# Attention: transposes of the negated maxima ahead of the matmuls for the sums of the weights

## The chip, the cores and the metric

The kernel runs on one core of one Trainium2 chip. The metric is the device time of one execution, in microseconds. The kernel before takes 1847.09 us in the median of 3 runs (1846.87 to 1848.96).

## What is computed

Two layers work on 2 x 1024 tokens of width 512, in fp32. Each adds an attention part and a feed-forward part to the normalised input. Only the second layer's attention matters here. It has 16 heads of width 32 and a causal mask:

```python
def _L1_attn_ref(x, W_qkv, b_qkv, W_out, b_out):
    ...
    qkv = x @ W_qkv.T + b_qkv
    q, k, v = jnp.split(qkv, 3, axis=-1)
    ...
    scores = jnp.einsum('bqhe,bkhe->bhqk', q, k) * scale
    causal = jnp.tril(jnp.ones((l, l), dtype=bool))
    scores = jnp.where(causal[None, None], scores, -jnp.inf)
    attn = jax.nn.softmax(scores, axis=-1)
    out = jnp.einsum('bhqk,bkhe->bqhe', attn, v)
    out = out.reshape(b, l, d)
    out = out @ W_out.T + b_out
    return out
```

## The kernel before

The kernel has three stages: the first layer (about 0 to 723 us), the second layer's attention (723 to 1230), and the second layer's feed-forward (to the end).

Attention works in 8 units, one for each batch and each group of four heads. The scores are computed twice. The first pass, `maxima` (L1033), puts queries on partitions: it multiplies q and k in PSUM pair tiles `m` (L1042, four heads, two heads to a pair), adds the mask on the diagonal (L1049) and takes the row maxima on VectorE (L1050). `shift_part` (L1062) negates the maxima on ScalarE and splits them into three bf16 parts, with GpSimd forming what is left. `shift_rows` (L1074) turns the parts around with four bf16 transposes on TensorE into the PSUM tile `px` (L1080), which VectorE copies to SBUF as `neg` (L1084).

The second pass, `weights` (L1086), puts keys on partitions: it multiplies k and q into the pair tiles `s` (L1095), adds the negated maxima with a three-row bf16 matmul of ones (L1101), takes the exponential on ScalarE into `pt` or `acc` (L1112), and sets what lies above the diagonal to zero on GpSimd (L1117). `gather` (L1126) multiplies the values with it into `o` (L1137, one group of 32 array columns per head) and adds `pt` onto `acc` on GpSimd (L1145, on VectorE near the end). `total` (L1152) sums `acc` over the keys with matmuls of ones into the PSUM tile `w` (L1157, again one group of 32 columns per head), and ScalarE copies it to `inv` (L1162). `divide` (L1164) takes reciprocals on VectorE in four quarters (L1167), and GpSimd multiplies the attention output with them (L1169).

`s`, `m`, `w` and `px` all come from `ps_wide`, a rotation of three PSUM tiles of two banks each. A tile's writer waits until the reader of the tile three places earlier in the rotation is done. A step without `w` and `px` takes s, s, m, m; one with both takes s, s, w, px, m, m.

The order of work is written out by hand in one loop (L1300). A unit has 12 steps n: four for the first half of the queries, eight for the second. Each step issues the second pass for its key block, what `put_mid` has noted for it, `gather` for the step before, what `put_after` has noted for it, the first pass for 13 steps ahead (`ahead`), and a part of a projection (`one_part`: two matmuls out of `pq`, `pv` or `po`, L990). `in_program_order` (L48) then holds TensorE, VectorE, ScalarE and GpSimd to the order of that list. `put_after` appends to a list for a step, and the list is worked off in the order in which it was filled:

```python
            for f, *args in after.pop(n, ()):
                f(*args)
```

`shift_rows` is noted at the steps 12u - 5 and 12u + 3, `total` at 12u + 7 and 12u + 15. So they meet in 14 steps: at 12u + 7 `total(u, 0)` with `shift_rows(u + 1, 0)`, and at 12u + 3 `total(u - 1, 1)` with `shift_rows(u, 1)`. In the step 12u + 7 the scores are 512 queries wide; in the step 12u + 3 they are 128 wide, and the `o` of the step before is 256 wide. In all of these steps but the last (in unit 7) a first pass 512 keys wide follows.

Of the kernel before, what the change touches and what calls it, by code (L numbers as in the profile page):

```python
# [35 lines left out]
def two_layers(ctx: ExitStack, tc: tile.TileContext, t: dict, out: bass.AP):  # L36
# [307 lines left out]
    with tc.tile_pool(name="a", bufs=1) as a:  # L344
# [415 lines left out]
        for n in range(NU - 1):  # L760
            u = 2 * n + 2
# [24 lines left out]
        for q, n in enumerate(((0, 2), (0, 4), (1, 2), (1, 4))):  # L786
            put0(*n, fwht_rows, q)
            for m in range(4):
                n, at = (0, (4, 5, 6, 6)[m]) if q == 0 else divmod(4 * q + 3 + m, 7)
# [101 lines left out]
        n, second_half = NU - 1, list(products_of(NU - 1, 1))  # L891
# [14 lines left out]
    with tc.tile_pool(name="b", bufs=1, reuse_waits="tile") as b:  # L906
# [91 lines left out]
        def project(u, m, n):  # L998


            bb, hg = units[u]

            def done(pq):
                if (u, m) not in qk:
                    qk[u, m] = b.tile([P, S], F32, tag=f"qk{m}", name=f"qk{m}_{u}", bufs=3)
                nc.scalar.activation(  # L1006
                    qk[u, m][:, n * TT : (n + 1) * TT], pq, AF.Identity,
                    bias=bqk[:, m * HG + hg : m * HG + hg + 1],
                )

            return piece(
                f"pq_{u}_{m}_{n}", lambda k: wqk[hg][:, k, m, :],
                lambda k: xt1[2 * bb + n][:, k, :], done,
            )

        def values(bb, n, j):


            def done(pv):
                if (bb, n, j) not in vals:  # L1020
                    vals[bb, n, j] = b.tile(
                        [P, D], F32, tag="v", name=f"v_{bb}_{n}_{j}", bufs=12
                    )
                nc.vector.tensor_add(vals[bb, n, j], pv, bv)

            return piece(
                f"pv_{bb}_{n}_{j}", lambda k: xt1[2 * bb + n][:, k, j * P : (j + 1) * P],
                lambda k: wv[:, k, :], done,
            )
# [170 lines left out]
        def put(n, *what):  # L1200
            fixed.setdefault(n, []).append(what)

        def put_mid(n, *what):

            middle.setdefault(n, []).append(what)

        def put_after(n, *what):

            after.setdefault(n, []).append(what)

        for u in range(len(units)):

            for half in range(2):
                n = per * u - ahead + (3, 11)[half]
                if half:
                    put(n + 1, larger, u)
                for m in range(3):
                    put_mid(n + 2 + m, shift_part, u, half, m)
                put_after(n + 5, shift_rows, u, half)
            if u:  # L1220
                lo = per * (u - 2) if u > 1 else -ahead
                for x in range(4):
                    rest.append((lo, per * u - ahead - 1, project(u, x // 2, x % 2)))
            if u > 1:
                put(per * (u - 2) - 1, load_qk, units[u][1])
            for j in range(2):
                n = per * u + 8 * j + 7
                if n < len(second):
                    put_after(n, total, u, j)
                    for q in range(4):  # L1230
                        put(n + q * 2 // 3, divide, u, j, q)
                else:
                    put(len(second) + 2, total, u, j)
        for x in range(4):
            rest.append((-ahead, x, values(0, 0, x)))
            rest.append((-ahead, 7 + x, values(0, 1, x)))
            for j in range(2):
                put(2 * x + j - 12, last_stats, 2 + x // 2, 2 * (x % 2) + j)
                put(2 * x - 9, last_row, 2 + x // 2, 2 * (x % 2) + j)
            put(2 * x - 10, last_norm, 2 + x // 2, x % 2)  # L1240
            rest.append((per, per * 4 + x, values(1, 0, x)))

            rest.append((per * 3 + 5 + x, per * 4 + 2 + x, values(1, 1, x)))
# [77 lines left out]
        n = len(second)  # L1321
# [14 lines left out]
    with tc.tile_pool(name="c", bufs=1, reuse_waits="tile") as c_:  # L1336
# [127 lines left out]
        for n in range(groups - 1):  # L1464

            end = n == groups - 2
            u = 2 * n + 2
# [22 lines left out]
        n = groups - 1  # L1490
# [144 lines left out]
```

## Time and profile before

| | |
|---|---|
| median of 3 runs | 1847.09 us (1846.87 to 1848.96) |
| the profiled execution | 1850.59 us |
| its span, first to last instruction | 1848.78 us |
| mean granted TensorE clock | 0.994 |
| matmuls of `w`, L1157 | 128 of 0.592 us (16 times `total`) |
| transposes into `px`, L1080 | 64 of 0.219 us (16 times `shift_rows`) |
| copy of `w` on ScalarE, L1162 | 16 of 0.585 us |
| copy of `px` on VectorE, L1084 | 16 of 0.424 us |
| exponential of a full pair, L1112 | 1.02 us |
| maxima of a full pair, L1050 | 1.22 us |

How to read the profile: PE is the matmul side of TensorE and PEld its weight loads, DVE is VectorE, ACT ScalarE, POOL GpSimd. A row of the timeline has the start in us from the span's start, the length in us, the engine, the line, the operation with the tile it writes and those it reads, the shape, and the number of instructions merged. A bracket gives the idle time of the engine before it and what ended it. An fp32 matmul is listed as two passes, so four heads give x8. Matmuls overlap: the time that a group holds TensorE is the distance from its start to the start of the next group, which is shorter than the row's length.

### The profile page before, as it was taken

Reading aid. Unit: us, or ns where it says so; the run is one execution under the profiler, and the core shown is the slowest. Engines: PE = TensorE matmul, PEld = TensorE weight load, DVE = VectorE, ACT = ScalarE, POOL = GpSimd, SP = SyncE. Lnnn points to the kernel's source line nnn. Section 1 sums busy time; section 2 is a strip of 40 time slices with the busy share of each in tenths; the row PEclk is TensorE's granted clock in tenths of the full one; section 3 lists DMA queues with packets and bytes.
Section 4 is the critical chain, followed back from the end, with each engine's and each line's share of the span. In section 5 each row is a group of like instructions: output and inputs, shape, how many; then the busy total and the mean of one; then the engine's idle time right before and its main releaser. Section 6 shows DMA issues by size and latency. Waiting matters only on the chain.

```text
span 1848.8 us, 18896 instructions
## 1 busy us (share of the span) xinstructions
PE 1798.2 (97%) x7348; PEld 918.6 (50%) x7348; DVE 1127.4 (61%) x1464; ACT 478.5 (26%) x683; POOL 821.1 (44%) x711
## 2 busy tenths in 40 slices
PE   6999999999999999999999999999999999999999
PEld 4446565655655564333333333333455555555544
DVE  3685444565543438565657656642768678768665
ACT  2322222122221102334333443412211221212120
POOL 4335364246552222467667756732244244343410
PEclk9999999999999999999999999999999999999999
DMA  6121111011101100000001000011101101211101
GB/s 228 35 80 34 35 35 38 31 46 35 35 23 34 35 7 23 1 12 12 13 1 35 12 12 1 24 46 34 35 23 57 57 23 58 91 35 46 46 1 46
DMA packets 29465, 68.12 MB, mean 37 GB/s; under 512 B 3392, under 2 KB 11584, under 8 KB 27840
## 3 DMA queue, kind: packets, MB, share of 16 engines
q1 hardware_dynamic: 28656, 66.61, 10.9%
q8 instruction: 59, 0.97, 0.2%
q10 hardware_dynamic: 720, 0.30, 0.1%
q14 instruction: 30, 0.25, 0.0%
HBM read 62.70 MB, written 4.19 MB: 36 GB/s over the span
## 4 chain that ended last, share of the span: by engine, by line
PE 88%; DVE 5%; POOL 2%; ACT 2%; issue 2%; DMA 1%; ACTq 0%; POOLq 0%; DVEq 0%
PE p_a L179 20%; PE p_c L179 19%; PE d L297 19%; PE pq L990 6%; PE m L1042 4%; PE s L1095 4%; PE o L1137 3%; PE po L990 3%; PE pv L990 3%; PE dr L1454 2%; POOL acc L1145 2%; PE w L1157 1%; DVE tops L1050 1%; PE pp L579 1%; PE s L1101 1%
## 5 line engine op out<-in xcount | busy, mean ns | idle before, releaser
L315 POOL TENSOR_TENSOR x<-x,de 128x512 f32<-128x512 f32 x87 | 125.9, 1462 | 298.4 <-DVE x L310 163.7
L1145 POOL TENSOR_TENSOR acc<-acc,pt 128x1024 f32<-128x1024 f32 (+3 forms) x138 | 233.7, 1719 | 0.0
L1050 DVE TENSOR_REDUCE tops<-m 128x2 f32<-128x1024 f32 (+2 forms) x192 | 180.8, 956 | 49.1 <-PE m L1042 44.7
L310 DVE TENSOR_TENSOR x<-x,d 128x512 f32<-128x512 f32 x145 | 99.3, 685 | 149.8 <-PE d L297 148.6
L1112 ACT ACTIVATE pt<-s 128x1024 f32<-128x1024 f32 (+3 forms) x160 | 115.1, 766 | 180.3 <-PE s L1101 167.1
L297 PE MATMUL d<-td,h 128*128 128x256 f32 x592 | 139.9, 380 | 2.2 <-DVE h L272 2.2
L297 PEld LDWEIGHTS d<-td,h 128*128 128x128 f32 x592 | 112.2, 190 | 46.2 <-issue 29.0
L990 PE MATMUL pq<-xt,wqk 128*128 128x512 f32 x256 | 125.1, 617 | 0.8 <-ACT qk L1006 0.8
L179 PE MATMUL p_a<-t_a,s_a 128*128 128x512 f32 x256 | 119.2, 610 | 2.1 <-DVE t_a L156 2.1
L179 PE MATMUL p_a<-xt,w 128*128 128x512 f32 x256 | 117.7, 603 | 0.7 <-ACT xt L136 0.7
L179 PE MATMUL p_c<-xt,s_c 128*128 128x512 f32 x256 | 115.2, 593 | 2.5 <-DVE e_c L224 1.4
L179 PE MATMUL p_a<-xt,s_a 128*128 128x512 f32 x256 | 116.6, 598 | 0.0
L179 PE MATMUL p_c<-xt,gu 128*128 128x512 f32 x256 | 114.9, 592 | 0.0
L179 PE MATMUL p_c<-t_c,s_c 128*128 128x512 f32 x256 | 114.6, 592 | 0.0
L1049 DVE TENSOR_TENSOR m<-m,mask 128x256 f32<-128x256 f32 x128 | 54.7, 427 | 98.2 <-PE m L1042 93.7
L1042 PE MATMUL m<-qk,qk 32*128 32x512 f32 (+3 forms) x768 | 107.7, 536 | 3.6 <-ACT acc L1112 3.0
L1095 PE MATMUL s<-qk,qk 32*128 32x512 f32 (+3 forms) x768 | 93.8, 532 | 3.7 <-ACT pt L1112 2.3
L172 POOL TENSOR_TENSOR s_c<-gu,s_c 128x512 f32<-128x512 f32 x16 | 20.4, 1275 | 135.9 <-PE p_c L179 135.9
L1117 POOL TENSOR_SCALAR_AFFINE_SELECT pt<-pt 128x256 f32<-128x256 f32 x112 | 48.4, 448 | 71.2 <-ACT pt L1112 70.6
L990 PEld LDWEIGHTS pq<-xt,wqk 128*128 128x128 f32 x256 | 44.5, 191 | 66.5 <-issue 62.1
L179 PEld LDWEIGHTS p_a<-xt,s_a 128*128 128x128 f32 x256 | 47.2, 190 | 57.1 <-issue 56.7
L179 PEld LDWEIGHTS p_c<-xt,s_c 128*128 128x128 f32 x256 | 48.5, 190 | 54.2 <-issue 52.9
(240 smaller groups left out, 3049.2 us busy)
## 6 DMA issues: line engine op xcount, KB each, us to landing
w<-in_W SPq DMA_DIRECT2D x32, 512.0 KB, 3.6
gu<-in_gu SPq DMA_DIRECT2D x32, 512.0 KB, 3.6
wd<-in_down SPq DMA_DIRECT2D x8, 1024.0 KB, 4.8
x<-in_x SPq DMA_DIRECT2D x16, 256.0 KB, 4.2
w2h<-in_W2q SPq DMA_DIRECT2D x4, 1024.0 KB, 11.7
xr<-in_x SPq DMA_DIRECT2D x16, 256.0 KB, 2.7
wqk<-in_WqkvT SPq DMA_DIRECT2D x16, 256.0 KB, 3.2
out_x<-x SPq DMA_DIRECT2D x16, 256.0 KB, 2.0
```

Source lines behind the costliest of these rows:

```text
L179: nc.tensor.matmul(pair[:, m, :], a[:, m, k, :], x[:, k, :], start=start and k == 0, stop=stop and k == 1, skip_group_check=True,)
L297: nc.tensor.matmul(out_[:, j, :], lhs[:, q, j * P : (j + 1) * P], rhs[:, q], start=m in (0, 1, 3, 4) and j == q == 0, stop=j == q == 1, sk ...
L310: nc.vector.tensor_add(r, r, out_)
L315: nc.gpsimd.tensor_add(r, r, u2[half])
L990: nc.tensor.matmul(got[0], lhs(k), rhs(k), start=(k == 0), stop=(k == KC - 1))
L1042: nc.tensor.matmul(pair[h // 2][:, h % 2, :e], q[rows, qt * P : (qt + 1) * P], k[rows, c * 512 : c * 512 + e], start=True, stop=True,)
L1049: nc.vector.tensor_add(d, d, mask.unsqueeze(1).to_broadcast([P, 2, P]))
L1050: nc.vector.tensor_reduce(out=tops[u][:, c, qt, 2 * p : 2 * p + 2], in_=pair[p][:, :, :e], axis=mybir.AxisListType.X, op=ALU.max,)
L1095: nc.tensor.matmul(pair[h // 2][:, h % 2, s:], k[rows, kt * P : (kt + 1) * P], q[rows, cols], start=True, stop=False,)
L1112: nc.scalar.activation(pt[:, :, s:], pair[p][:, :, s:], AF.Exp, scale=1.0 / math.sqrt(HD))
L1137: nc.tensor.matmul(po[rows, s:], v[:, rows], pts[h // 2][:, h % 2, s:], start=(kt == 0), stop=last, tile_position=(0, h * HD),)
L1145: eng.tensor_add(acc[:, :, s:], acc[:, :, s:], pt[:, :, s:])
```

## The change

`total` is no longer noted while the units are walked through. It is collected in a list, and noted for its steps after all `shift_rows` are. In a step that has both, `shift_rows` is now issued first and `total` behind it. Steps that have one of the two stay as they are, and the steps themselves are the same. With the order, the places in the rotation of PSUM tiles change: such a step takes s, s, px, w, m, m.

```diff
+        sums_at = []
         for u in range(len(units)):
 
             for half in range(2):
...
             for j in range(2):
+
                 n = per * u + 8 * j + 7
                 if n < len(second):
-                    put_after(n, total, u, j)
+                    sums_at.append((n, total, u, j))
                     for q in range(4):
                         put(n + q * 2 // 3, divide, u, j, q)
                 else:
                     put(len(second) + 2, total, u, j)
+        for what in sums_at:
+            put_after(*what)
```

## The prediction

> **What bounds the kernel now.** I read the page first, for the busy engine and the chain that ended last.
>
> ```profile
> span 1848.8 us, 18896 instructions
> PE 1798.2 (97%) x7348; PEld 918.6 (50%) x7348; DVE 1127.4 (61%) x1464; ACT 478.5 (26%) x683; POOL 821.1 (44%) x711
> PE 88%; DVE 5%; POOL 2%; ACT 2%; issue 2%; DMA 1%; ACTq 0%; POOLq 0%; DVEq 0%
> ```
>
> TensorE is busy for 97% of the span and carries 88% of the chain. So a microsecond saved in its queue counts, unless another engine is the limit at that place. Then the busy time by stretch, inside attention (723 to 1230 us):
>
> ```profile
> 860.00:920.00 60.00, 59.01 (x400) 21.27 (x397) 37.37 (x53) 22.41 (x36) 40.80 (x43) 1.00 0.03 10
> 920.00:980.00 60.00, 59.01 (x399) 21.25 (x396) 36.08 (x51) 23.92 (x38) 40.79 (x42) 1.00 0.04 10
> ```
>
> The columns after the length are PE, PEld, DVE, ACT and POOL. One unit of four heads lasts about 61 us, PE is busy for 59.0 of 60, and POOL, the next, for 40.8. PE's own short stalls are hidden in that busy time, because matmuls overlap and a pair that waits lies under its neighbour. They have to be read from starts. So I took the timeline at the two kinds of step that hold both w and px. First the wide one (query rows 512 wide), then the narrow one (scores only 128 wide), and then an ordinary step without either.
>
> ```profile
> 783.83 1.06 PE L1137 MATMUL o<-pt,v 128*32 128x512 f32 x8
> 784.71 1.04 PE L1157 MATMUL w<-acc,ones 128*32 128x512 f32 x8
> 785.68 0.40 PE L1080 MATMUL px<-identb,parts 128*128 128x128 bf16 x4
> 785.82 0.59 ACT L1162 COPY inv<-w 128x512 f32<-128x512 f32 x1
> 786.01 1.57 PE L1042 MATMUL m<-qk,qk 32*128 32x512 f32 x8
> 786.12 0.42 DVE L1084 COPY neg<-px 128x512 bf16<-128x512 bf16 x1 [3.33 <-PE px L1080]
> 787.51 1.98 PE L990 MATMUL pq<-xt,wqk 128*128 128x512 f32 x4
> ```
>
> ```profile
> 824.82 1.07 PE L1157 MATMUL w<-acc,ones 128*32 128x512 f32 x8 [0.48 <-DVE tops L1050]
> 825.82 0.40 PE L1080 MATMUL px<-identb,parts 128*128 128x128 bf16 x4
> 825.94 0.58 ACT L1162 COPY inv<-w 128x512 f32<-128x512 f32 x1 [1.50 <-PE w L1157]
> 826.15 1.56 PE L1042 MATMUL m<-qk,qk 32*128 32x512 f32 x8
> 827.64 1.98 PE L990 MATMUL pq<-xt,wqk 128*128 128x512 f32 x4
> ```
>
> ```profile
> 795.75 1.07 PE L1137 MATMUL o<-pt,v 128*32 128x512 f32 x8
> 796.75 1.15 PE L1042 MATMUL m<-qk,qk 32*128 32x512 f32 x8
> 797.83 1.98 PE L990 MATMUL pv<-wv,xt 128*128 128x512 f32 x4
> ```
>
> What to see: m of the same shape (eight passes of 512) holds PE from its start to the next group's start for 797.83 - 796.75 = 1.08 us where nothing is in its way. It takes 787.51 - 786.01 = 1.50 us in the wide step and 827.64 - 826.15 = 1.49 in the narrow one. The cause is the rotation of three PSUM pairs. A step takes s, s, w, px, m, m in that order, so the second m pair gets the buffer of the tile that stands first after s, which is w. It waits for ScalarE's copy of w, which ends at 785.82 + 0.59 = 786.41 (narrow: 826.52), although m could have had it at 786.01. That is 0.42 us (narrow 0.41) of bare wait on the bottleneck engine.
>
> **The change part by part.** The program orders of the two kernels, laid side by side, differ in PE alone: in 14 steps the four transposes of px come ahead of w's matmuls. No instruction is added, and DVE, ACT, POOL and the DMA queue keep theirs in order. Of the 14 steps, 7 are wide (PE's w at 784.71 and then each 62 us), 6 narrow (824.82 and so on), and one is a narrow one in the tail (1190).
>
> 1. The second m pair now takes px's buffer and waits for VectorE's copy of px. In the wide step px starts in w's place after o. Behind o an instruction of another array shape starts 796.75 - 795.75 = 1.00 after o's start, so px starts at 784.83. The copy starts 786.12 - 785.68 = 0.44 later and takes 0.42, so it ends at 785.69. VectorE stood idle for 3.33 us before that copy, so it is free. m needs the buffer only at about 786.16, and the copy is covered by w's matmuls with 0.47 us to spare. The stall of 0.42 goes.
>
> 2. The price is the order o, px, w, m. Here a rule speaks against the change. The row: px starts 785.68 - 784.71 = 0.97 after w in the wide step, and w starts only 784.71 - 783.83 = 0.88 after o, while m behind o takes 1.00. So w right behind o gets in 0.12 early, since both use 32-column groups. The Trainium skill (TensorEngine Tiling (Array Packing), Key Properties) says that changing the tiling mode drains TensorE, changing the tile within one mode doesn't. Before, o and w share a mode and px and m are one change each. After, px stands between o and w, one more drain in each wide step. The rule gives no price; the rows do: 0.12 for w's lost early start, and 0.03 for its first weight load (w holds 1.00 in the narrow step, where it starts on a drained array, against 0.97). So o 1.00, px 0.33 (786.01 - 785.68), w 1.00: m starts at 783.83 + 2.33 = 786.16, 0.15 later than now, and the next group at 787.24 in place of 787.51: -0.27. If the drain were free it would be -0.42. A w group directly behind a bf16 transpose is not in this trace. The nearest row is m behind px, 0.33, and I take it. A gain below nothing is excluded since the number of changes grows; from above, all eight weight loads of w bare, 8 x 0.110 us (the group of w's LDWEIGHTS) = 0.88, is the worst.
>
> 3. In the narrow step px, not w, is what waits for the preceding maxima on VectorE, at the same 824.82. The array is drained there anyway. px 0.33 and w 1.00 put m at 826.15 as today, and 0.41 goes whole.
>
> 4. The wait that takes the removed one's place is on the next step's first score pair: it now gets w's buffer. ScalarE's copy starts 1.11 us after w (785.82 - 784.71), so 785.16 + 1.11 + 0.59 = 786.86. The scores come at 789.43 - 0.27 = 789.16. m (1.08) and pq (1.91) cover it with 2.3 us; without pq there are still 0.4. ScalarE idles 4.49 us ahead of its next exponential, so nothing is queued behind the later copy. The second score pair waits for the first maximum, at most 0.15 later (about 788.55), also in time. The reciprocals come behind both maxima and move with them.
>
> 5. The tail step has no m. There the second score pair is the one that waits for w's copy: s holds 1.70 us against 1.29 elsewhere. The same sum gives -0.28, but the reciprocals, and VectorE's sums behind them, start about 0.4 later, so between -0.28 and +0.2. I take -0.2, nearer the PE rows.
>
> What the saved time runs into: POOL's sums form a closed queue after each wide step, but that queue begins with a mask that waits for an exponential (POOL idle 6.9 us before it at 792), and the exponential waits for scores on PE. It starts earlier by as much as PE. The wait for maxima ahead of the narrow step starts from m on PE as well.
>
> Sum: 7 x 0.27 = 1.9, 6 x 0.41 = 2.5, tail 0.2: 4.6 us. The profiled execution took 1850.59 us (span 1848.78), so it would be 1846.0. It lies 3.5 above the median of the runs, 1847.09; taken from that, 1842.5.
>
> **Rivals.**
> - The saving is absorbed. What speaks for it: PE waits 0.48 us for VectorE's maxima ahead of each narrow step, and POOL's queue reaches up to an o in the first unit. If the wide steps' 1.9 stayed there, only 2.7 are left: 1844.4. Against it: both queues start from PE, as above.
> - Slower, by the drain: if w behind a transpose must load all its weights bare, each of the 14 steps pays 0.88, or 12.3, against 4.6 saved: 1854.8. It decides from 0.33 us per step upward (4.6 / 14). Against it: m behind the same transposes starts in 0.33, with its loads run ahead.
> - The change doesn't do what it says: m's second pair really waits for the exponential of its step. Then the extra drains stay, 7 x 0.15: 1848.1. Against it: in the wide step that exponential ended at 785.86 and in the narrow one at 824.45, long before the pair moved, while the copy's end fits both.
>
> **How the numbers follow.** About 0.2%, 3.7 us, is what a measurement of this kernel can tell from no change. Forecast 0.70, absorbed 0.16, drain 0.09, no effect 0.05. The forecast's own spread is some 1 us. The runs lie 2.1 apart, and a stretch of 3.4 us at a granted clock of 0.51 (809.2 in this trace) costs about 0.7 on the pq it hits (2.57 for 1.91); where it falls may differ. So of 0.70, 0.62 lies under 1843.4; with a little of the absorbed case faster is 0.65, the same 0.25, slower 0.10. The range goes from 1841.0 (drain free, 7 x 0.15 more, and half a microsecond of spread) to 1846.0, which takes in the absorbed case and leaves out the other two.
>
> **What would show it.** In the profile after, px at about 1.00 behind o in the wide steps, w 0.33 behind px, m 1.08 in place of 1.50 in both kinds, the copy of w behind m's start, and the scores without a wait for that copy. It is wrong if w starts later than 0.4 behind px, if m still holds 1.5, or if a new gap of some 0.3 us opens ahead of the scores, of o, or of the next narrow step's px.

## The result

The changed kernel takes 1844.52 us in the median of 14 runs (1841.11 to 1846.34), the kernel before 1847.95 beside it (14 runs, 1846.87 to 1849.49). The ratio is 0.9979, with a 95% interval of 0.9971 to 0.9987: 3.4 us gained. In a second session it took 1843.59 in the median of 10 runs, at a ratio of 0.9974 (0.9965 to 0.9983).

The profiled execution took 1841.11 us with a span of 1839.4, 9.4 less than the one of before. That is more than the runs differ by, and more than the change is worth, so the page's span must not be read as the effect. First the page, then the two kinds of step.

```profile
span 1839.4 us, 18901 instructions
PE 1788.5 (97%) x7348; PEld 911.7 (50%) x7348; DVE 1122.8 (61%) x1464; ACT 478.6 (26%) x683; POOL 820.1 (45%) x711
```

The wide step after, in the timeline:

```profile
782.21 1.07 PE L1137 MATMUL o<-pt,v 128*32 128x512 f32 x8
783.20 0.40 PE L1080 MATMUL px<-identb,parts 128*128 128x128 bf16 x4
783.53 1.06 PE L1157 MATMUL w<-acc,ones 128*32 128x512 f32 x8
783.64 0.42 DVE L1084 COPY neg<-px 128x512 bf16<-128x512 bf16 x1 [2.47 <-PE px L1080]
784.53 1.14 PE L1042 MATMUL m<-qk,qk 32*128 32x512 f32 x8
784.66 0.58 ACT L1162 COPY inv<-w 128x512 f32<-128x512 f32 x1 [0.42 <-PE w L1157]
785.60 1.98 PE L990 MATMUL pq<-xt,wqk 128*128 128x512 f32 x4
```

The copy of px ends at 784.06, before m starts, and the copy of w runs beside m. The row of m has shrunk from 1.57 to 1.14, and m holds PE for 785.60 - 784.53 = 1.07 us where it held 1.50. From the start of o to that of px it takes 0.99 where it took 0.88 from o to w, and w starts 0.33 behind px. From o to pq the step takes 3.39 us, before 787.51 - 783.83 = 3.68: 0.29 less. The narrow step after:

```profile
820.41 0.64 PE L1137 MATMUL o<-pt,v 128*32 128x256 f32 x8
821.53 0.38 PE L1080 MATMUL px<-identb,parts 128*128 128x128 bf16 x4 [0.48 <-DVE tops L1050]
821.84 1.06 PE L1157 MATMUL w<-acc,ones 128*32 128x512 f32 x8
822.84 1.14 PE L1042 MATMUL m<-qk,qk 32*128 32x512 f32 x8
823.91 1.98 PE L990 MATMUL pq<-xt,wqk 128*128 128x512 f32 x4
```

Now px bears the wait of 0.48 for VectorE's maxima that w bore, m again holds 1.07, and from the first of the pair to pq it takes 2.38 in place of 827.64 - 824.82 = 2.82: 0.44 less. In the view of waits of PE over attention, w stood before and px stands after, and no other line has grown:

```profile
PE w L1157 <- DVE tops L1050: 2.9, 6, 0.5
PE px L1080 <- DVE tops L1050: 0.5, 1, 0.5
```

```profile
PE px L1080 <- DVE tops L1050: 3.4, 7, 0.5
PE m L1042 <- ACT acc L1112: 3.0, 8, 0.7
```

All 7 wide and all 6 narrow steps read the same to 0.02 us. From one wide step to the next a unit takes 61.10 us after (841.20 to 902.30, from the scores' start) and 61.83 before (844.93 to 906.76). The 0.73 are the 0.29 and the 0.44 of the two steps, so nothing is taken back in between.

**Where the other 4.6 us of the profile come from.** Both traces contain stretches of 3.4 us, or twice that, at half the granted clock. The stretch table of before and of after, at three such places and at one without (the eighth field is the granted clock):

```profile
809.20:812.65 3.45, 3.45 (x18) 1.70 (x19) 1.23 (x3) 2.18 (x4) 3.45 (x6) 0.51 0.00 0
1215.40:1218.85 3.45, 3.45 (x8) 1.17 (x4) 1.90 (x4) 0.00 (x0) 1.29 (x2) 0.51 1.01 425
```

```profile
806.00:810.00 4.00, 3.76 (x31) 1.54 (x24) 2.13 (x5) 2.52 (x4) 4.00 (x6) 1.00 0.01 4
1052.70:1056.10 3.40, 3.40 (x18) 1.54 (x15) 1.31 (x3) 2.05 (x4) 3.40 (x6) 0.50 0.00 0
```

Before has them at 31, 75, 809, 1215 and 1321 us, after at 29, 1053 and 1312. The starts of the same matmuls, set against each other, show the difference by place: 1.6 us are gained by 100 us, where the two kernels are the same, 1.4 more than the two steps explain in the unit around 809, and 1.65 at 1215. That is 4.6, and with the 4.8 of the steps it makes 9.4. Near 1055 both lose 1.4 us, which cancels: after to a stretch, before to a maximum on VectorE that took 4.60 us in place of 0.71 (shown in the last section).

The stretches are no property of either kernel, since their number differs between executions of one kernel. The second profile of the changed kernel has 23.9 us at half clock and a span of 1843.0, the first 13.7 us and 1839.4: 3.6 us for three stretches more, 1.2 each. Each run's mean granted clock lies between 0.991 and 0.998, and the times follow it. Over the 133 runs of all kernels here that have a clock on record, one common slope and a level for each kernel leave 0.84 us of scatter, and the slope is 1.32 us (plus or minus 0.13) for each 0.001 of clock. A stretch of 3.41 us at half clock is 3.41 / 2 / 1848 = 0.0009 of clock, so again about 1.2 us. Below, "at equal clock" means this level, with a 95% interval. For the changed kernel (24 runs) it is 4.6 (plus or minus 0.4) under the kernel before (49 runs).

### The profile page after: what moved, and what is told of

Its sections match the earlier page's. It is cut to its first block, busy times and chain, and to the rows that moved or that the text cites. A ratio compares the mean times of both kernels' runs of the same rounds, so it can differ in the third digit from the quotient of the medians.

```text
span 1839.4 us, 18901 instructions
## 1 busy us (share of the span) xinstructions
PE 1788.5 (97%) x7348; PEld 911.7 (50%) x7348; DVE 1122.8 (61%) x1464; ACT 478.6 (26%) x683; POOL 820.1 (45%) x711
## 4 chain that ended last, share of the span: by engine, by line
PE 88%; DVE 5%; POOL 3%; ACT 2%; issue 2%; DMA 0%; SPq 0%; ACTq 0%; DVEq 0%; POOLq 0%
PE p_a L179 20%; PE p_c L179 20%; PE d L297 19%; PE pq L990 6%; PE m L1042 4%; PE s L1095 4%; PE o L1137 3%; PE po L990 3%; PE pv L990 3%; PE dr L1458 2%; POOL acc L1145 2%; PE w L1157 1%; DVE tops L1050 1%; PE pp L579 1%; ACT acc L1112 1%
## 5 line engine op out<-in xcount | busy, mean ns | idle before, releaser
L1042 PE MATMUL m<-qk,qk 32*128 32x512 f32 (+3 forms) x768 | 102.2, 535 | 3.7 <-ACT acc L1112 3.0
```

Of the source, the lines that this page charges most:

```text
L1042: nc.tensor.matmul(pair[h // 2][:, h % 2, :e], q[rows, qt * P : (qt + 1) * P], k[rows, c * 512 : c * 512 + e], start=True, stop=True,)
```

## The experiments

The theory: the gain is the second m pair's wait for w's copy, which needs both the order and the place in the rotation, and the price is one more change of array shape in a wide step. The rivals: the order alone does it, the rotation alone does it, or the gain is partly absorbed by other engines' queues.

**The order alone.** px is issued ahead of w, but w's tile is taken first, so m still gets w's buffer.

```diff
+            todo = after.pop(n, ())
+            if len(todo) == 2:
+                (_, *a), (_, *c) = todo
+                pw = ps_wide(f"w_{a[0]}_{a[1]}")
+                shift_rows(*c)
+                total(*a, pw)
+                todo = ()
```

> The 14 steps issue px ahead of w as in the changed kernel, but the PSUM rotation stays as before (w's tile is taken first, px's second), so the second m pair still gets w's buffer. Theory (the gain is the wait for w's copy, gone because px's buffer comes free first): no gain, a loss. In a wide step px starts about 785.0 (it waits for the first exponential now), w 785.34, w's copy ends 787.04, m holds 0.75 + 1.06 = 1.81 us in place of 1.50: +0.6 per wide step, about 0 per narrow step (px runs while w waits for the maxima, m holds 1.8 from 0.33 earlier). Sum +4.5 us over the kernel before. Rival (the order itself brings the gain, since px and its copy are early): -3 to -5 us as in the changed kernel.

Measured: 1850.73 us, ratio 1.0014 (1.0005 to 1.0023), at equal clock 3.5 slower (plus or minus 0.6). The wide step of its timeline (its lines lie one later):

```profile
783.50 0.38 PE L1081 MATMUL px<-identb,parts 128*128 128x128 bf16 x4
783.81 1.06 PE L1158 MATMUL w<-acc,ones 128*32 128x512 f32 x8
784.81 1.90 PE L1042 MATMUL m<-qk,qk 32*128 32x512 f32 x8
784.94 0.59 ACT L1163 COPY inv<-w 128x512 f32<-128x512 f32 x1 [0.58 <-PE w L1158]
785.58 0.30 PEld L1042 LDWEIGHTS m<-qk,qk 32*128 32x128 f32 x4 [0.48 <-ACT inv L1163]
786.64 1.98 PE L990 MATMUL pq<-xt,wqk 128*128 128x512 f32 x4
```

m holds 1.83 us, since its second pair waits for a copy that ends at 785.53, 0.72 behind m's start. The weight loads of that pair name it: they start at 785.58, released by ScalarE's `inv`. The order by itself is a loss: w now stands directly ahead of m, so its copy ends 0.72 behind m's start where it ended 0.40 behind (786.41 against 786.01), and m still needs it.

**The rotation alone.** w is issued ahead of px, but px's tile is taken first.

```diff
+                px = ps_wide(f"px_{c[0]}_{c[1]}")
+                total(*a)
+                shift_rows(*c, px)
```

> The 14 steps issue w ahead of px as before, but px's tile is taken first in the PSUM rotation and w's second, so the second m pair gets px's buffer. Theory: in a wide step w now waits for the first exponential (785.0 in place of 784.71), px follows at 785.98, its copy ends 786.85 and m still stalls, holding 1.65: +0.45. In a narrow step w no longer waits for the maxima (824.27 in place of 824.82), px at 825.27, m holds 1.64 from 825.60: -0.40. Sum 7 x 0.45 - 6 x 0.40 = +0.7 us. Rival (the rotation alone brings the gain, the order is a price): 0.15 per wide step better than the changed kernel, about -5.5 us.

Measured: 1848.28 us, ratio 1.0003 (0.9994 to 1.0012), at equal clock 0.3 slower (plus or minus 0.6). Its wide and its narrow step:

```profile
785.05 1.06 PE L1158 MATMUL w<-acc,ones 128*32 128x512 f32 x8 [0.20 <-POOL acc L1146]
786.05 0.40 PE L1081 MATMUL px<-identb,parts 128*128 128x128 bf16 x4
786.38 1.71 PE L1042 MATMUL m<-qk,qk 32*128 32x512 f32 x8
786.49 0.42 DVE L1085 COPY neg<-px 128x512 bf16<-128x512 bf16 x1 [3.74 <-PE px L1081]
786.96 0.30 PEld L1042 LDWEIGHTS m<-qk,qk 32*128 32x128 f32 x4 [0.29 <-DVE neg L1085]
788.02 1.98 PE L990 MATMUL pq<-xt,wqk 128*128 128x512 f32 x4
...
823.36 1.06 PE L1158 MATMUL w<-acc,ones 128*32 128x512 f32 x8
824.35 0.40 PE L1081 MATMUL px<-identb,parts 128*128 128x128 bf16 x4
824.68 1.72 PE L1042 MATMUL m<-qk,qk 32*128 32x512 f32 x8
824.79 0.42 DVE L1085 COPY neg<-px 128x512 bf16<-128x512 bf16 x1 [0.98 <-PE px L1081]
```

m still stalls, holding 1.64, now for the copy of px, which stands directly ahead of it; the weight loads of the second pair are released by `neg`. Wide steps are 0.55 longer than before, narrow ones 0.44 shorter, because w no longer waits for the maxima. The two nearly cancel.

The bracket names GpSimd for w's wait in the wide step, but the wait that is new there is for the first exponential, whose buffer w now takes. That exponential ends at 784.91, and w starts 0.14 later, at 785.05, when a sum on GpSimd happens to end too. In the wide step of unit 6 the two come apart: the exponential ends at 1157.17 and w starts at 1157.31, again 0.14 later, while GpSimd's sum runs on to 1158.31.

Neither half of the change gains what the whole does; both rivals fall. The steps alone sum to +4.2 for the order (six wide steps +0.63 and the one of unit 6 +0.47, narrow steps -0.08, the tail +0.5) and to +1.2 for the rotation (+0.55, +0.36, -0.44, +0.2), 0.7 and 0.9 above the levels at equal clock. That is outside the intervals, and where it goes stays open; the unit lengths agree with the steps (61.95 against 61.83 for the rotation).

**Wide steps only, narrow steps only.** The list of a step is reversed in one kind of step.

```diff
-            for f, *args in after.pop(n, ()):
+            todo = after.pop(n, ())
+            for f, *args in todo[::-1] if n % per == 7 else todo:
```

> Only the 7 wide steps (12u + 7) have px ahead of w; narrow steps stay as before. Theory: 7 x 0.28 = -2.0 us, read from the profile as 0.28 less from o's start to the next group behind m in each wide step, all of it still there at the end of attention. Rival (wide steps' gain is absorbed by GpSimd's queue, which begins behind them): the steps are shorter but the PE is not ahead after the unit, about -0.3 us.

> Only the 7 narrow steps (12u + 3) have px ahead of w; wide steps stay as before. Theory (the two kinds of step are independent and add up): each narrow step 0.44 shorter (4.00 us from the scores' start to the group behind m, in place of 4.44), the one in the tail about 0.1: -2.7 us at the same granted clock, which with the -1.7 of the wide steps alone makes the -4.4 of the changed kernel. Rival (the gain ahead of VectorE's maxima is partly lost again at the next wait for them): -1.5 us or less, and a longer o ahead of the next px.

Measured: wide only 1849.16 us, ratio 0.9993 (0.9983 to 1.0004), narrow only 1845.44, ratio 0.9982 (0.9974 to 0.9991). The median of wide only lies above the kernel before, its ratio below. Its runs had the lowest mean clock of all (0.9941 against 0.9947). At equal clock it gains 1.8 (plus or minus 0.6), narrow only 2.6 (0.6). Together these are 4.4, against 4.6 for the changed kernel, so the kinds add up. In both profiles the changed steps read as in the changed kernel (0.29 and 0.44 less) and the others as before. The rival that the gain is absorbed falls for both.

**Another place for px in the wide steps.** To price the change of array shape, px is put ahead of o, so that o and w (both in groups of 32 columns) are neighbours again. Narrow steps stay as in the changed kernel.

```diff
-                put_after(n + 5, shift_rows, u, half)
+                (put_after if half else put_mid)(n + 5, shift_rows, u, half)
...
+            for f, *args in todo[::-1] if n % per == 3 else todo:
```

> Narrow steps as in the changed kernel (px, then w behind o); in the wide steps px is issued ahead of o (s, px, o, w, m), so that o and w stand side by side again. Theory (a wide step of the changed kernel pays 0.13 to 0.15 us for one more change of array shape between o and w): o 0.33 behind px, w 0.88 behind o, m 1.08, a wide step gains 0.42 in place of 0.28; in all about -5.5 us against the kernel before, 0.9 better than the changed kernel. Rival (the change of shape costs nothing, the 0.13 lie in something else, such as w's first weight load behind px): no better than the changed kernel.

> px ahead of o in the wide steps once more, beside the changed kernel on one chip. Theory: 0.06 us per wide step less than the changed kernel (4.62 against 4.68, as its first profile showed: w waits there for the first exponential), 0.4 to 0.8 us less at the same clock. Rival: no difference from the changed kernel.

> The changed kernel once more, on the chip of the others of this call. Theory: -4.4 us against the kernel before at the same granted clock; without regard to the clock anywhere between -2.5 and -5.5, since runs differ by up to 5 us with the number of half-clock stretches. Rival (the median gap of 3.4 is the true one): -3.4 at the same clock too.

Measured: 1843.03 us, ratio 0.9967 (0.9955 to 0.998), and on the second chip 1841.27, 0.9962 (0.9949 to 0.9974), beside 0.9974 for the changed kernel. At equal clock it gains 5.4 (plus or minus 0.6) against 4.6 (0.4) for the changed kernel; the difference is 0.7 (plus or minus 0.65). Its wide step:

```profile
782.39 0.40 PE L1080 MATMUL px<-identb,parts 128*128 128x128 bf16 x4
782.49 1.94 ACT L1112 ACTIVATE pt<-s 128x1024 f32<-128x1024 f32 x2 [0.59 <-PE s L1101]
782.72 1.06 PE L1137 MATMUL o<-pt,v 128*32 128x512 f32 x8
783.65 1.07 PE L1157 MATMUL w<-acc,ones 128*32 128x512 f32 x8
784.65 1.14 PE L1042 MATMUL m<-qk,qk 32*128 32x512 f32 x8
```

From px to m it takes 784.65 - 782.39 = 2.26, in the changed kernel 2.32 from o to m: 0.06 less and not the 0.13 expected. w starts 0.93 behind o and not 0.88, because its buffer is that of the first exponential, which ends at 783.51. In the one wide step where the exponential is early (unit 6) w has its 0.88 and 0.97, and the step is 0.14 shorter than in the changed kernel. So the change of shape costs what the rows of before said, and half of it comes back as a wait. At equal clock this version gains most of those tried; its lead over the changed kernel is only just clear of the scatter.

**px behind m in the narrow steps**, with px ahead of o in the wide ones:

```diff
+            late_px = todo[1:] if len(todo) == 2 and n % per == 3 else ()
...
                 do_first(n + ahead)
+            for f, *args in late_px:
+                f(*args)
```

> In wide steps px ahead of o (as in px_first); in narrow steps px behind m, next to the projection, so that no copy stands between s and m in the PSUM rotation and px needs no change of array shape towards pq. Theory (the wait for a copy and the changes of shape are all that the order costs): a narrow step 0.50 + 1.12 + 1.00 + 1.07 + 0.25 = 3.95 us from the scores to the projection against 4.00 in the changed kernel; the later copy of px, behind both maxima on VectorE, ends at about 829.1 and is needed at 830. Sum -5.5 us against the kernel before at the same clock, -5.2 for px_first. Rival (px's copy behind the maxima is late for the next step's scores or for the next second score pair, which now waits for the second maximum): a gap of 0.2 us or more ahead of the next s, and no better than px_first.

Measured: 1843.46 us, ratio 0.997 (0.9959 to 0.9982), at equal clock 4.7 better than before (plus or minus 0.7). That is no better than px ahead of o alone: 0.6 worse, plus or minus 0.9. Its narrow step and the next scores:

```profile
885.48 1.14 PE L1042 MATMUL m<-qk,qk 32*128 32x512 f32 x8
886.55 0.40 PE L1080 MATMUL px<-identb,parts 128*128 128x128 bf16 x4
886.65 2.35 DVE L1050 TENSOR_REDUCE tops<-m 128x2 f32<-128x1024 f32 x2 [2.32 <-PE m L1042]
886.78 1.94 PE L990 MATMUL pq<-xt,wqk 128*128 128x512 f32 x4
888.65 1.54 PE L1095 MATMUL s<-qk,qk 32*128 32x512 f32 x8
888.92 0.41 DVE L1084 COPY neg<-px 128x512 bf16<-128x512 bf16 x1
...
890.34 0.43 PE L1137 MATMUL o<-pt,v 128*32 128x128 f32 x8
```

px next to the projection takes 0.23 in place of 0.31 (both use the whole array, so no change of shape lies between them), and the step is 0.08 shorter than the changed kernel's. But s then holds 890.34 - 888.65 = 1.69 us in place of 1.29: its second pair waits for the second maximum, which VectorE ends at 889.0. From this narrow step to the next wide one it takes 21.37 us against 21.29 in the changed kernel, and the whole unit 61.13 (843.11 to 904.24) against 61.04 with px ahead of o alone (842.63 to 903.67). The rival was right here. It is a wait that the changed kernel does not have.

## Why the prediction held, step by step

- **The stall of m and its cause**: right, 0.43 in the wide steps (forecast 0.42) and 0.42 in the narrow ones (0.41). The two halves of the change, taken alone, show that it is the buffer's reader that decides, and that order and rotation are needed together.
- **The price of the extra change of shape**: forecast 0.15 in a wide step, measured 0.14: from o to m it takes 784.53 - 782.21 = 2.32, before 786.01 - 783.83 = 2.18. With the 0.43 this leaves 0.29 gained (forecast 0.27). w started 0.33 behind px, as the nearest row, m behind px, said. That m's weight loads run ahead there was a wrong reading: loads and matmuls of m both start at 786.01 in the trace. In narrow steps px holds 0.31, which makes their gain 0.44 in place of 0.41.
- **The new waits**: right; neither the scores nor the second score pair wait in the changed kernel.
- **The rivals**: all three fall. The gain is not absorbed, since a unit is shorter by what its two steps gain. The drain does not cost 0.88 per step, since w starts 0.33 behind px. And m's second pair does not wait for the exponential, since it holds 1.07.
- **The tail**: forecast 0.2 gained, between 0.28 gained and 0.2 lost. From the scores at 1188.75 (after 1181.09) to the o two steps later it is 7.23 in place of 7.32, so 0.1.
- **The sum**: forecast 4.6. By the steps 7 x 0.29 + 6 x 0.44 + 0.1 = 4.8; at equal clock 4.6; by the medians 3.4 and, in the second session, 1843.59 against 1848.49, 4.9. That forecast and level agree to 0.1 is closer than the interval of 0.4 and in part luck.
- **The predicted time**, 1842.5: the median was 1844.52, 2.0 above. Of this 0.9 is that the kernel before itself came out at 1847.95 in place of 1847.09. The rest is that these two medians lie 3.4 apart and not 4.6, which the second session did not repeat. The term that was mis-sized is the spread: the forecast gave its own as 1 us and one half-clock stretch as 0.7 us on the one group it hits. A stretch costs 1.2 to 1.4, and the two profiles of the changed kernel hold four and seven times 3.41 us of it. So its 14 runs spread by 5 us (1841.11 to 1846.34), and a median moves by 1 to 2 us: by 0.9 between the two sessions of the changed kernel, by 1.8 between the two of px ahead of o.

## What to carry to other kernels

In a rotation of buffers, ask which reader each later writer waits for: the tile that stands one full turn ahead of a stalled matmul should be the one whose copy is finished first, so issue the producer with the early copy first, and let the other producer's matmuls cover that copy. Here px's copy is done 0.86 us after px starts (783.20 to 784.06), and w's 1.00 of matmuls stand behind px. Try order and rotation apart, because either alone can lose. When runs of a kernel differ by more than the effect sought, compare step lengths in the traces and read times at equal granted clock.

## What was not expected of the hardware

- The half-clock stretches fall at a handful of places, though not in every run: near 30, 75, 808, 1055, 1182, 1212 and 1317 us in the ten profiles of this study. At 808 and 1055 PE has just stalled for an exponential that GpSimd's sums held up, in units whose step has no projection (m of 128 columns holds 1.52 us there, although it holds 0.43 where nothing is in its way), and at 1212 scores hold 2.37 us. What decides whether a stretch falls in a given run was not tried.
- At 809 a stretch cost about 1.4 us: the first unit, counted from the scores of its wide step to those of the next, takes 62.39 us before and 60.28 after, 2.11 apart, of which the two steps explain 0.73. At 1053 one cost 1.4 us as well. With it the unit there takes 61.69 us in the first profile of the changed kernel (1026.21 to 1087.90), without it 60.27 in the second (1028.08 to 1088.35).
- In the profile of before, that unit takes 62.40 us without any stretch, 1.4 more than the steps explain. There a small VectorE instruction, the maximum over the two halves of the keys (L1060), took 4.60 us, and a score pair waited for the VectorE work behind it. The row of before, then that of after:

```profile
1057.68 4.60 DVE L1060 TENSOR_TENSOR tops<-tops 128x16 f32<-128x16 f32 x1
1051.46 0.71 DVE L1060 TENSOR_TENSOR tops<-tops 128x16 f32<-128x16 f32 x1
```

In the ten profiles 10 of the 80 executions of this instruction took 3.7 to 4.6 us, the others 0.2 to 1.4. Each of the long ones ended 0.02 to 0.03 us after GpSimd had come to the end of a run of instructions without a gap (here at 1062.26). They cost PE 1.4 us here, 0.6 at 932 us in the profiles of wide only and narrow only, and nothing at 995 in that of before. So this is a second cause of scatter, which the clock does not show. What sets it off was not tried.
